# An eight-block performer and mixture-of-experts kernel: the final stage moved beside the last two experts, feature matmuls in 64-row pairs, one one-hot buffer

## The chip, the cores and the metric

The kernel runs on one core of one Trainium2 chip. A core has a matmul engine (TensorE, PE in the tables, with its weight loads as PEld), a vector engine (VectorE, DVE), a scalar engine for activations (ScalarE, ACT), a general engine (GpSimd, POOL) and a queue engine (SyncE, SP). SP, ACT and POOL also issue DMAs. Every engine executes its own queue in order. Matmul results go to PSUM, which has eight banks of 512 float32 columns on 128 partitions; all other tiles lie in SBUF. The metric is the device time of one execution in microseconds (us); the median of several runs is what counts.

## The reference

The input is 4096 tokens of 256 numbers in 8 sequences of 512. Two layers follow, each of the form `x = x + layernorm(f(layernorm(x)))`:

```python
# layer 1: performer attention and an MLP
xp   = einsum('bhnd,md->bhnm', x * norm, proj)      # 16 heads of 16, 64 features
qp   = ratio * (exp(xp - diag - max over m) + eps)          # queries
kp   = ratio * (exp(xp - diag - max over n and m) + eps)    # keys
ctx  = einsum('bhnm,bhnd->bhmd', kp, v)
out  = einsum('bhnm,bhmd->bhnd', qp, ctx) / denom
x    = layer_norm(video + out @ Wo.T + bo, g2, be2)
x    = layer_norm(x + relu(x @ W1.T + b1) @ W2.T + b2, g3, be3)
# layer 2: 8 experts, each takes the 512 tokens that score highest for it
scores = softmax(xf @ gate_w.T)
vals, idx = top_k(scores.T, 512)
y    = layernorm(xf[idx]) * ln_w + ln_b
out  = (gelu(y @ fc1.T + b1s) @ fc2.T + b2s) * vals
xf   = xf.at[idx].add(out)
```

A token may belong to several experts or to none. What leaves the kernel is `x1 + layernorm(xf)` after all experts have added, where `x1` is the result of the first layer.

## The kernel before, in words

The 4096 tokens are worked in NB = 8 blocks of 512; a block has NT = 4 tiles of 128 tokens (t). A scheduler decides the order of the instructions in each engine's queue from the program order and its own estimates; waits are put in wherever a tile, a PSUM bank or a DRAM table is still in use. So the source order and the queue order differ in places.

**Blocks.** Three generators are stepped in turn, so that block b's attention, block b-1's MLP and block b-2's gate are interleaved (L517 to L522). In `attention(b)`, the normalised input is transposed (L159), projected to kT and qT (L231), and the raw features are computed per t: for each half c of the model dimension, one matmul of 128 rows times `pj`, a block-diagonal matrix with 8 copies of proj, into one PSUM bank `px` of 128x512 (L281 for k, L346 for q). DVE reads each bank twice: a maximum (L285, L351) and a subtraction (L286, L353). For k, the maximum over all tokens goes through a POOL reduction (L295) to `nstab`, then ACT takes exponentials (L319), DVE scales them (L323) and PE sums them with v into `pc` (L329). For q, ACT takes exponentials (L357), PE transposes them (`ptq`, L367), ACT copies them out (L372), and PE multiplies with the context (`po`, L382). `mlp(b)` holds the matmuls `ph` (L448) and `pm` (L459); `gate(b)` makes `x1` in SBUF, its layer norm `xf`, which SP stores into the DRAM table `acc` (L478), the gate scores and the rows `yg`, which ACT's queue stores into the DRAM table `xg` (L512).

**PSUM.** Three pools share the eight banks: `ps_mm` (4: matmul results), `ps_tr` (2: transposes), `ps_sm` (2: small results).

**Selection.** A bisection over the scores finds each expert's threshold (L573 to L607); scans give each chosen token a slot. `tokens_of(e)` turns slots into the token list `idx` of an expert: DVE builds a one-hot matrix `hot` of 128x4096 (L662), PE sums it in 32 matmuls into `pi` (L667), DVE makes `idx` from it (L673, L675). `hot` has two buffers.

**Experts.** For expert e, POOL gathers 512 rows from `xg` in four indirect DMAs (L681), PE transposes them, eight matmul pairs `phe` give the hidden layer (L697), ACT applies GELU to each (L702), four groups of 16 PE instructions give `pwe` (L709), DVE adds the bias and multiplies by the kept score (L712, L713), and POOL scatters the four row groups with addition into `acc` (L716). Scatters to one table wait for each other. The weights of expert e+1 are loaded, and its tokens found and gathered, while expert e works.

**Final stage.** After the last scatter, SP loads each of the 8 blocks of `acc` as a tile `z` (L735), the helper `ln_plain` computes its layer norm (DVE statistics L130 and L131, POOL's rs in two instructions L132 and L133, DVE scaling L139), DVE adds `x1` (L739) and ACT's queue stores the block to `out` (L740).

## Time and profile before

| what | value |
|---|---|
| runs | 1170.94, 1167.29, 1170.92, 1169.33 us; median 1170.12 |
| profiled execution | 1166.58 us; span of its work 1164.9 us |
| granted TensorE clock, mean | 0.911 of full |
| blocks, about 30 to 790 us | a block every 94 us or so (transposes from 79.3 to 644.9 us for blocks 1 to 7) |
| selection, about 790 to 860 us | hardly any matmul |
| experts, about 860 to 1106 us | 29.0 us from one expert to the next |
| rest, 1106 to 1165 us | no matmul |

Share of the span by engine: PE 83%, DVE 52%, ACT 24%, POOL 20%. The page of the profile divides the span into 40 slices and gives the busy tenths of each engine:

```profile
PE   2989988998998998899899899882179999999900
DVE  2765467647737737755764773646743110111146
POOL 3010013004103102200300400313042233333222
```

One digit is 29 us. The notch near the 26th digit is the selection; the last two digits are the final stage, in which DVE works and PE doesn't. A mean over the span says little here: each stage has to be read by itself. Matmuls are pipelined, so that a busy PE isn't PE at its peak; where a row gives an engine's idle time, the releaser behind the arrow is the instruction that ended it.

### The profile page before, as it was taken

To read this page: it belongs to the slowest core of one execution; us is meant where nothing else is said; L and a number is where in the kernel's file an instruction comes from. 1 tells how busy PE (TensorE), PEld (TensorE's weight loads), DVE (VectorE), ACT (ScalarE), POOL (GpSimd) and SP (SyncE) were. 2 spreads that over 40 slices of the span, in tenths; PEclk is the share of its full clock that TensorE was granted. 3 is DMA by queue.
4 is the path that set the end of the run, shared out by engine and by line. 5 is a ranking of instruction groups with operands and counts; after the bars stand their busy time and mean duration, and the time that the engine had idled before them with its cause. 6 is when DMAs were issued, how large, how long until landed. Compare 5 with 4: busy or idle time off the path is not lost. (4 is left out here: it accounts for less than half of the span.)

```text
span 1164.9 us, 12047 instructions
## 1 busy us (share of the span) xinstructions
PE 968.2 (83%) x4452; PEld 668.4 (57%) x4452; DVE 602.3 (52%) x1696; ACT 276.0 (24%) x490; POOL 235.2 (20%) x239
## 2 busy tenths in 40 slices
PE   2989988998998998899899899882179999999900
PEld 1575874684585586477458558562047766666600
DVE  2765467647737737755764773646743110111146
ACT  0332332332312323233232241210011121222200
POOL 3010013004103102200300400313042233333222
PEclk9999999998999999999999999895569999999955
DMA  6000001001000100100000010012313434443163
GB/s 223 1 1 1 1 1 49 8 1 36 19 1 0 55 1 1 55 1 1 18 19 1 1 38 1 0 37 84 134 38 91 105 70 108 109 109 73 18 183 115
DMA packets 41177, 52.62 MB, mean 45 GB/s; under 512 B 2720, under 2 KB 37536, under 8 KB 40864
## 3 DMA queue, kind: packets, MB, share of 16 engines
q1 hardware_dynamic: 17248, 24.12, 6.2%
q10 hardware_dynamic: 17728, 19.22, 5.0%
q0 software_dynamic: 6144, 8.52, 4.5%
q8 instruction: 35, 0.57, 0.2%
q14 instruction: 22, 0.18, 0.0%
HBM read 34.95 MB, written 16.91 MB: 45 GB/s over the span
## 5 line engine op out<-in xcount | busy, mean ns | idle before, releaser
L448 PE MATMUL ph<-xaT,w_sb 128*128 128x512 f32 x256 | 131.3, 641 | 20.1 <-DVE kp L286 16.4
L459 PE MATMUL pm<-w_sb,hT 128*128 128x256 f32 x512 | 122.9, 399 | 0.0
L697 PE MATMUL phe<-yT,w1e 128*128 128x512 f32 x256 | 117.8, 620 | 1.6 <-ACT yT L160 1.2
L712 DVE TENSOR_TENSOR o<-pwe,b2s_sb 128x256 f32<-128x256 f32 x32 | 13.6, 425 | 198.8 <-PE pwe L709 198.8
L459 PEld LDWEIGHTS pm<-w_sb,hT 128*128 128x128 f32 x512 | 101.7, 201 | 18.1 <-issue 3.8
L709 PE MATMUL pwe<-w2e,hTe 128*128 128x256 f32 x512 | 111.8, 379 | 0.0
L709 PEld LDWEIGHTS pwe<-w2e,hTe 128*128 128x128 f32 x512 | 97.3, 190 | 16.6 <-issue 3.8
L448 PEld LDWEIGHTS ph<-xaT,w_sb 128*128 128x128 f32 x256 | 51.2, 206 | 83.4 <-issue 71.2
L697 PEld LDWEIGHTS phe<-yT,w1e 128*128 128x128 f32 x256 | 50.2, 199 | 64.1 <-issue 60.5
L716 POOL DMA_INDIRECT acc<-o,idx x32 | 50.4, 1575 | 164.0 <-DVE o L713 75.9
L267 POOL TENSOR_TENSOR xn<-xn,rows_sb 128x1024 f32<-128x1024 f32 x8 | 19.2, 2405 | 303.0 <-PE pt_x L159 303.0
L452 ACT ACTIVATE hT<-ph,cols_sb 128x512 f32<-128x512 f32 x64 | 43.8, 685 | 128.2 <-PE ph L448 121.8
L281 PE MATMUL pxk<-pj,kT 128*128 128x512 f32 x128 | 67.0, 636 | 0.0
L463 DVE TENSOR_TENSOR r<-pm,r 128x256 f32<-128x256 f32 x32 | 13.6, 425 | 101.3 <-PE pm L459 101.3
L329 PEld LDWEIGHTS pc<-v_aug,kp 128*128 128x128 f32 x512 | 61.2, 194 | 6.6 <-issue 3.8
L382 PEld LDWEIGHTS po<-ctxb,qpT 128*128 128x128 f32 x512 | 61.8, 192 | 3.7 <-issue 3.3
L702 ACT ACTIVATE hTe<-phe,cols_sb 128x512 f32<-128x512 f32 x64 | 44.0, 687 | 83.1 <-PE phe L697 83.1
L346 PE MATMUL pxq<-pj,qT 128*128 128x512 f32 x128 | 61.7, 600 | 0.0
L382 PE MATMUL po<-ctxb,qpT 128*128 128x34 f32 x512 | 61.0, 270 | 0.0
L372 ACT ACTIVATE qpT<-ptq 128x512 f32<-128x512 f32 x64 | 34.9, 595 | 108.0 <-PE ptq L367 108.0
L329 PE MATMUL pc<-v_aug,kp 128*128 128x34 f32 x512 | 59.8, 276 | 0.0
L319 ACT ACTIVATE kp<-kp,nstab 128x256 f32<-128x256 f32 x128 | 52.7, 495 | 16.0 <-DVE nstab L297 16.0
(184 smaller groups left out, 1478.9 us busy)
## 6 DMA issues: line engine op xcount, KB each, us to landing
w2e<-in_f ACTq DMA_DIRECT2D x8, 1024.0 KB, 6.0
w1e<-in_f SPq DMA_DIRECT2D x8, 1024.0 KB, 5.2
xg<-yg ACTq DMA_DIRECT2D x8, 528.0 KB, 3.0
x<-in_x_in SPq DMA_DIRECT2D x8, 512.0 KB, 3.9
acc<-xf SPq DMA_DIRECT2D x8, 512.0 KB, 2.8
z<-acc SPq DMA_DIRECT2D x8, 512.0 KB, 6.0
out<-z ACTq DMA_DIRECT2D x8, 512.0 KB, 3.0
w_sb<-in_w SPq DMA_DIRECT2D x2, 1024.0 KB, 12.0
```

What stands on the lines that cost most here:

```text
L281: nc.tensor.matmul(px.rearrange("p h m -> p (h m)"), kT[:, c, ts(t, P)], pj.rearrange("p h m -> p (h m)"), start=True, stop=True,)
L319: nc.scalar.activation(kp[:, :, h, :], kp[:, :, h, :], AF.Exp, bias=nstab[:, h : h + 1])
L329: nc.tensor.matmul(pc[:, hp, :, :].rearrange("p a d -> p (a d)"), kp[:, t, pair, :].rearrange("p h m -> p (h m)"), v_aug[:, t, pair, :].re ...
L346: nc.tensor.matmul(px.rearrange("p h m -> p (h m)"), qT[:, c, ts(t, P)], pj.rearrange("p h m -> p (h m)"), start=True, stop=True,)
L382: nc.tensor.matmul(po[:, 2 * hp : 2 * hp + 2, :].rearrange("p a d -> p (a d)"), qpT[:, hp, :], ctxb[:, hp, :, :].rearrange("p a d -> p (a ...
L448: nc.tensor.matmul(ph, w1_sb[:, c, ts(f, P)], xaT[:, c, :], start=(c == 0), stop=(c == KD - 1),)
L452: nc.scalar.activation(hT[:, f, :], ph, AF.Relu, bias=cols_sb[:, C_B1 + f : C_B1 + f + 1])
L459: nc.tensor.matmul(pw, hT[:, f, ts(t, P)], w2_sb[:, f, :], start=(f == 0), stop=(f == NF - 1),)
L697: nc.tensor.matmul(ph, w1e[:, c, ts(f, P)], yT[:, c, :], start=(c == 0), stop=(c == KD - 1),)
L702: nc.scalar.activation(hT[:, f, :], ph, AF.Gelu_apprx_tanh, bias=cols_sb[:, col : col + 1])
L709: nc.tensor.matmul(pw, hT[:, f, ts(j, P)], w2e[:, f, :], start=(f == 0), stop=(f == NF - 1))
L716: nc.gpsimd.indirect_dma_start(out=acc[:, :], out_offset=bass.IndirectOffsetOnAxis(ap=idx[:, j : j + 1], axis=0), in_=o[:, j, :], in_offse ...
```

## The change

Three parts are changed.

First, the raw features. `pj` holds 8 heads of 16 rows each, so that its rows 0 to 63 are zero in the columns of heads 4 to 7, and rows 64 to 127 in those of heads 0 to 3. The new helper `raw_features` leaves these zero halves out: for each c it issues two matmuls, one from the rows 0 to 63 and one from the rows 64 to 127, each with 256 columns. The two row halves (g) write to two banks of a two-bank tile `pxs`, which comes from a pool of its own, `ps_px`, with two buffers. DVE then reads one bank for each g, as before twice. The views `heads` and `head_cols` put the heads in their old places. To make room in PSUM, `ps_tr` is gone (its tiles come from `ps_mm`), `ps_mm` has 3 banks instead of 4 and `ps_sm` 1 instead of 2.

Second, `hot` has one buffer instead of two.

Third, the final stage. `gate(b)` now also stores `x1` into a DRAM table `x1d` through SP. The experts 6 and 7 (`late`) gather, beside their own rows `y`, the rows of `x1d` and those of `acc` as they stand after all earlier experts (`x1g`, `zg`). After each row group's result `o`, DVE adds it to `zg`, and the layer norm and the addition of `x1g` follow in place; these rows are then scattered to `out` itself, without addition. The blocks are finished as whole blocks from `acc` too: blocks 0 to 3 during expert 6 and blocks 4 to 7 during expert 7, at fixed places in the loops over f and j, with the scaling on ACT instead of DVE (`finish_z`), loads and stores both on SP, and four buffers `z`. The block results are wrong for the rows that experts 6 and 7 still change; the scatters to `out`, which come after the block stores, put the right rows in their place, those of expert 7 after those of expert 6. Expert 7 no longer scatters to `acc`.

```diff
     dram = ctx.enter_context(tc.tile_pool(name="dram", bufs=1, space=DRAM))
-    ps_mm = ctx.enter_context(tc.tile_pool(name="ps_mm", bufs=4, space=PSUM))
-    ps_tr = ctx.enter_context(tc.tile_pool(name="ps_tr", bufs=2, space=PSUM))
-    ps_sm = ctx.enter_context(tc.tile_pool(name="ps_sm", bufs=2, space=PSUM))
+    ps_px = ctx.enter_context(tc.tile_pool(name="ps_px", bufs=2, space=PSUM))
+    ps_mm = ctx.enter_context(tc.tile_pool(name="ps_mm", bufs=3, space=PSUM))
+    ps_sm = ctx.enter_context(tc.tile_pool(name="ps_sm", bufs=1, space=PSUM))
...
     acc = dram.tile([T, D], F32, name="acc")
+    x1d = dram.tile([T, D], F32, name="x1d")
...
         for c in range(KD):
-            pt = ps_tr.tile([P, TB], F32, tag="tr", name=f"pt_{tag}_{c}")
+            pt = ps_mm.tile([P, TB], F32, tag="mm", name=f"pt_{tag}_{c}")
             for t in range(NT):
...
+        HG = HC // 2
+        def heads(t, g):
+            return t.rearrange("p (c g i) m -> p g c i m", c=KD, g=2)[:, g, :, :, :]
+        def head_cols(t, g):
+            return t.rearrange("p (c g i) -> p g c i", c=KD, g=2)[:, g, :, :]
+        def raw_features(qT, t, tag):
+            pxs = ps_px.tile([P, 2, KD, HG, M], F32, tag="px", name=tag)
+            for c in range(KD):
+                for g in range(2):
+                    gs = slice(g * 64, (g + 1) * 64)
+                    nc.tensor.matmul(
+                        pxs[:, g, c, :, :].rearrange("p h m -> p (h m)"),
+                        qT[gs, c, ts(t, P)],
+                        pj[gs, g * HG : (g + 1) * HG, :].rearrange("p h m -> p (h m)"),
+                        start=True, stop=True,
+                    )
+            return pxs
...
             for t in range(NT):
-                for c in range(KD):
-                    hs = slice(c * HC, (c + 1) * HC)
-                    px = ps_mm.tile([P, HC, M], F32, tag="mm", name=f"pxk_{b}_{t}_{c}")
-                    nc.tensor.matmul(
-                        px.rearrange("p h m -> p (h m)"), kT[:, c, ts(t, P)],
-                        pj.rearrange("p h m -> p (h m)"), start=True, stop=True,
-                    )
-                    nc.vector.tensor_reduce(mxk[:, t, hs], px, AX.X, ALU.max)
+                pxs = raw_features(kT, t, f"pxk_{b}_{t}")
+                for g in range(2):
+                    nc.vector.tensor_reduce(
+                        head_cols(mxk[:, t, :], g), pxs[:, g, :, :, :], AX.X, ALU.max
+                    )
                     nc.vector.tensor_tensor(
-                        kp[:, t, hs, :], px,
-                        diagk[:, t, hs].unsqueeze(2).to_broadcast([P, HC, M]),
+                        heads(kp[:, t, :, :], g), pxs[:, g, :, :, :],
+                        head_cols(diagk[:, t, :], g).unsqueeze(3).to_broadcast([P, KD, HG, M]),
                         ALU.subtract,
...
                 qd = a2.tile([P, H, M], F32, tag="qd", name=f"qd_{b}_{t}")
-                for c in range(KD):
-                    hs = slice(c * HC, (c + 1) * HC)
-                    px = ps_mm.tile([P, HC, M], F32, tag="mm", name=f"pxq_{b}_{t}_{c}")
-                    nc.tensor.matmul(
-                        px.rearrange("p h m -> p (h m)"), qT[:, c, ts(t, P)],
-                        pj.rearrange("p h m -> p (h m)"), start=True, stop=True,
-                    )
-                    sh = small.tile([P, HC], F32, tag="sh", name=f"sh_{b}_{t}_{c}")
-                    nc.vector.tensor_reduce(sh, px, AX.X, ALU.max)
-                    nc.vector.tensor_tensor(sh, sh, diagq[:, t, hs], ALU.add)
+                pxs = raw_features(qT, t, f"pxq_{b}_{t}")
+                for g in range(2):
+                    sh = small.tile([P, KD, HG], F32, tag="sh", name=f"sh_{b}_{t}_{g}")
+                    nc.vector.tensor_reduce(sh, pxs[:, g, :, :, :], AX.X, ALU.max)
+                    nc.vector.tensor_tensor(sh, sh, head_cols(diagq[:, t, :], g), ALU.add)
                     nc.vector.tensor_tensor(
-                        qd[:, hs, :], px, sh.unsqueeze(2).to_broadcast([P, HC, M]),
+                        heads(qd, g), pxs[:, g, :, :, :],
+                        sh.unsqueeze(3).to_broadcast([P, KD, HG, M]),
                         ALU.subtract,
...
                 for g in range(2):
-                    pt = ps_tr.tile([P, 4, P], F32, tag="tr", name=f"ptq_{b}_{t}_{g}")
+                    pt = ps_mm.tile([P, 4, P], F32, tag="mm", name=f"ptq_{b}_{t}_{g}")
                     for i in range(4):
...
                 at = ats.pop(t)
-                pt = ps_tr.tile([P, KD, P], F32, tag="tr", name=f"pta_{b}_{t}")
+                pt = ps_mm.tile([P, KD, P], F32, tag="mm", name=f"pta_{b}_{t}")
                 for c in range(KD):
...
             nc.gpsimd.tensor_tensor(x1b, r1, x0, ALU.add)
+            nc.sync.dma_start(
+                x1d[b * TB : (b + 1) * TB, :].rearrange("(t p) d -> p t d", p=P), x1b
+            )
             yield
...
     W = 2 * P
-    pT = ps_tr.tile([P, 2, P], F32, tag="tr", name="pT")
+    pT = ps_mm.tile([P, 2, P], F32, tag="mm", name="pT")
     for k in range(2):
...
-    pv = ps_tr.tile([P, 2, NC // 2, E], F32, tag="tr", name="pslot")
+    pv = ps_mm.tile([P, 2, NC // 2, E], F32, tag="mm", name="pslot")
     for k in range(2):
...
         nc.vector.tensor_scalar(num[:, :, 0, :], num[:, :, 0, :], pcol, None, ALU.mult)
-        hot = ep.tile([P, P, NC], BF, tag="hot", name=f"hot_{e}")
+        hot = ep.tile([P, P, NC], BF, tag="hot", name=f"hot_{e}", bufs=1)
         nc.vector.tensor_tensor(
...
-    def expert(e, idx, y):
+    LATE = 2
+    def rows_of(table, idx, name):
+        g = ep.tile([P, NJ, D], F32, tag=name[:2], name=name)
+        for j in range(NJ):
+            nc.gpsimd.indirect_dma_start(
+                out=g[:, j, :], out_offset=None, in_=table[:, :],
+                in_offset=bass.IndirectOffsetOnAxis(ap=idx[:, j : j + 1], axis=0),
+                bounds_check=T - 1, oob_is_err=True,
+            )
+        return g
+    def scatter(table, idx, j, src, op=None):
+        kw = {} if op is None else {"compute_op": op}
+        nc.gpsimd.indirect_dma_start(
+            out=table[:, :],
+            out_offset=bass.IndirectOffsetOnAxis(ap=idx[:, j : j + 1], axis=0),
+            in_=src, in_offset=None,
+            bounds_check=T - 1, oob_is_err=True, **kw,
+        )
+    def load_z(b):
+        z = ep.tile([P, NT, D], F32, tag="z", name=f"z_{b}", bufs=4)
+        nc.sync.dma_start(
+            z, acc[b * TB : (b + 1) * TB, :].rearrange("(t p) d -> p t d", p=P)
+        )
+        return z
+    def finish_z(b, z):
+        mv, rs = ln_stats(z, NT, f"z{b}")
+        nb = small.tile([P, NT], F32, tag="nb", name=f"nb_{b}")
+        nc.vector.scalar_tensor_tensor(nb, mv[:, :, 0], -1.0, rs, ALU.mult, ALU.mult)
+        for t in range(NT):
+            nc.scalar.activation(
+                z[:, t, :], z[:, t, :], AF.Identity,
+                bias=nb[:, t : t + 1], scale=rs[:, t : t + 1],
+            )
+        nc.vector.tensor_tensor(z, z, x1[:, b * NT : (b + 1) * NT, :], ALU.add)
+        nc.sync.dma_start(
+            out[b * TB : (b + 1) * TB, :].rearrange("(t p) d -> p t d", p=P), z
+        )
+    idxs = {0: tokens_of(0)}
+    ys = {0: gather(0, idxs[0])}
+    zs = {}
+    for e in range(E):
+        if e + 1 < E:
+            ws[e + 1] = load_expert(e + 1)
+            idxs[e + 1] = tokens_of(e + 1)
+            ys[e + 1] = gather(e + 1, idxs[e + 1])
+        idx, y = idxs[e], ys.pop(e)
         w1e, w2e = ws.pop(e)
+        late = e >= E - LATE
+        if late:
+            x1g = rows_of(x1d, idx, f"x1g_{e}")
+            zg = rows_of(acc, idx, f"zg_{e}")
+        if e == E - LATE:
+            for b in range(NB // 2):
+                zs[b] = load_z(b)
         yT = ep.tile([P, KD, CAP], F32, tag="yT", name=f"yT_{e}")
...
+            if late and f in (4, 7):
+                b = (NB // 2 if e == E - 1 else 0) + f // 7
+                finish_z(b, zs.pop(b))
+                if e == E - LATE:
+                    zs[b + 4] = load_z(b + 4)
         o = ep.tile([P, NJ, D], F32, tag="o", name=f"o_{e}")
...
             )
-            nc.gpsimd.indirect_dma_start(
-                out=acc[:, :],
-                out_offset=bass.IndirectOffsetOnAxis(ap=idx[:, j : j + 1], axis=0),
-                in_=o[:, j, :], in_offset=None,
-                bounds_check=T - 1, oob_is_err=True, compute_op=ALU.add,
-            )
-    idxs = {0: tokens_of(0)}
-    ys = {0: gather(0, idxs[0])}
-    for e in range(E):
-        if e + 1 < E:
-            ws[e + 1] = load_expert(e + 1)
-            idxs[e + 1] = tokens_of(e + 1)
-            ys[e + 1] = gather(e + 1, idxs[e + 1])
-        expert(e, idxs[e], ys.pop(e))
-    for b in range(NB):
-        z = ep.tile([P, NT, D], F32, tag="z", name=f"z_{b}", bufs=NB - 2)
-        nc.sync.dma_start(
-            z, acc[b * TB : (b + 1) * TB, :].rearrange("(t p) d -> p t d", p=P)
-        )
-        ln_plain(z, z, NT, f"z{b}")
-        nc.vector.tensor_tensor(z, z, x1[:, b * NT : (b + 1) * NT, :], ALU.add)
-        nc.scalar.dma_start(
-            out[b * TB : (b + 1) * TB, :].rearrange("(t p) d -> p t d", p=P), z
-        )
+            if e < E - 1:
+                scatter(acc, idx, j, o[:, j, :], ALU.add)
+            if late:
+                zj = zg[:, j : j + 1, :]
+                nc.vector.tensor_tensor(zj, zj, o[:, j : j + 1, :], ALU.add)
+                ln_plain(zj, zj, 1, f"l{e}_{j}")
+                nc.vector.tensor_tensor(zj, zj, x1g[:, j : j + 1, :], ALU.add)
+            if e == E - LATE and j in (1, 3):
+                b = 2 + j // 2
+                finish_z(b, zs.pop(b))
+                zs[b + 4] = load_z(b + 4)
+            if e == E - 1:
+                if j in (0, 1):
+                    finish_z(6 + j, zs.pop(6 + j))
+                if j == 1:
+                    for i in range(NJ):
+                        scatter(out, idxs[e - 1], i, zg6[:, i, :])
+                    scatter(out, idx, 0, zg[:, 0, :])
+                if j >= 1:
+                    scatter(out, idx, j, zg[:, j, :])
+        if late:
+            zg6 = zg
...
```

Unchanged lines are left out at "...".

## The prediction

> **What bounds the kernel now.** I read the busy table first, then equal stretches of the span with the busy time of each engine, then the timelines of single engines.
>
> ```profile
> span 1164.9 us, 12047 instructions
> PE 968.2 (83%) x4452; PEld 668.4 (57%) x4452; DVE 602.3 (52%) x1696; ACT 276.0 (24%) x490; POOL 235.2 (20%) x239
> ...
> 330.00:430.00 100.00, 92.31 (x451) 65.55 (x451) 62.11 (x169) 27.70 (x52) 16.30 (x17) 0.96 0.05 17
> 1050.00:1090.00 40.00, 39.71 (x131) 23.99 (x130) 3.46 (x8) 10.70 (x16) 12.01 (x9) 1.00 0.29 55
> 1110.00:1130.00 20.00, 0.00 (x0) 0.00 (x0) 9.80 (x34) 0.00 (x0) 4.11 (x5) 0.50 0.66 201
> 1130.00:1165.00 35.00, 0.00 (x0) 0.00 (x0) 23.29 (x72) 0.00 (x0) 7.60 (x12) 0.50 0.37 129
> ```
>
> The columns after the stretch are PE, weight loads, DVE, ACT and POOL, then the granted clock. Three stages show: the attention and MLP blocks (30 to 790 us), where PE works 92 of 100 us; the experts (860 to 1106), where PE works 39.7 of 40; and a tail without any matmul. PE's last group begins at 1091.81 and takes 13.98, so it ends at 1105.8 and 59.1 us of tail follow. Of these, 8 pass until the last scatter lands, 4 load the first block, and 42.8 (1117.84 to 1160.6) are the eight blocks' statistics, scaling and addition.
>
> ```profile
> 406.82 1.88 PE L346 MATMUL pxq<-pj,qT 128*128 128x512 f32 x4
> 408.54 1.88 PE L448 MATMUL ph<-xaT,w_sb 128*128 128x512 f32 x4
> ...
> 413.74 7.15 PE L459 MATMUL pm<-w_sb,hT 128*128 128x256 f32 x32
> 420.73 1.88 PE L346 MATMUL pxq<-pj,qT 128*128 128x512 f32 x4
> ```
>
> A feature chunk (one t, two matmuls, four PE instructions) holds PE for 408.54 - 406.82 = 1.72 us, 0.43 for 512 columns. A 256-column instruction takes (420.73 - 413.74)/32 = 0.218. Each group is seen 0.16 longer than it holds PE: that is the pipe's emptying, now hidden by the next group.
>
> **The feature matmuls.** There are 8 blocks x 4 t x 2 (k and q) = 64 chunks. Each becomes four matmuls of 64 rows and 256 columns, eight instructions. One after the other they take 8 x 0.218 = 1.75, so nothing is won (+0.03). If the two row halves run at once, neighbours overlap only where the half changes: the order is half 0 twice, half 1 twice, and so on, so eight instructions fill five places, 5 x 0.218 = 1.09, or -0.63. With every pair together it would be 0.87, or -0.85. No matmul of this trace has 64 rows, so this is bounded, not read. Changing between whole and halved arrays may empty the pipe twice, 2 x 0.16 = +0.32. The ends for 64 chunks are thus -0.85 x 64 = -54 and +0.35 x 64 = +22 us. I take five places and one emptying, -0.47 a chunk, since the weight loads (0.19 each, overlapped) leave room for it.
>
> The Trainium skill speaks on both sides in "TensorEngine Tiling (Array Packing)", Key Properties: tiles load and multiply independently, but changing the tiling mode drains the engine. No row here shows either; the first half of the rule would give -54 and the second would add 64 x 0.32 = 20 us to it.
>
> PE time isn't block time. In the k part DVE is the slower one:
>
> ```profile
> 396.24 1.95 PE L448 MATMUL ph<-xaT,w_sb 128*128 128x512 f32 x4 [2.73 <-DVE kp L286]
> ...
> 394.81 0.68 DVE L285 TENSOR_REDUCE mxk<-pxk 128x8 f32<-128x512 f32 x1
> 401.99 0.24 DVE L293 TENSOR_REDUCE mxt<-mxk 128x16 f32<-128x64 f32 x1
> ```
>
> DVE reads the chunks without a gap from 394.81 to 401.99, and only then come the maximum, ACT's exponentials and the matmuls of pc (410.25). Today PE waits 2.73 for a bank in ps_mm; in the changed kernel the features have banks of their own (two chunks), so ph runs on, but chunk 3 must wait until DVE has read chunk 1. In the new DVE order all of yg's statistics stand earlier, which removes most of a 1.25 us wait for rs_g; I let DVE gain about 1.2 there. PE then does chunk 3, pv, ph 6, pxq 0 and ph 7 and reaches pc at about 406.9, 3.3 earlier than now. Behind it the three q chunks lie in dense PE work: 3 x 0.63 = 1.9. Against this, transposes and matmuls now share three banks instead of six and the small results have one instead of two: I charge 0.8 a block, the 0.3 us waits that the pta and pw rows already show, some three more of them. Emptying takes 1.1 (seven chunks at 0.16). That is 3.3 + 1.9 - 0.8 - 1.1 = 3.3 a block, times 7.5 (block 0 starts without MLP work to fill): **-25 us**, with ends -45 and +15, as DVE's chain caps the one and hides some of the other. DVE's two reads (0.69 and 0.68) keep their 512 elements.
>
> **One one-hot buffer.** hot of expert 1 must now wait for pi of expert 0 (846.79 + 2.08 = 848.9), and in the new DVE order idx of expert 0 stands behind it. It was done at 849.44; now 848.9 + 0.2 + 2.28 + 0.15 = 851.5. The gathers, transposes and first expert matmul wait for it: **+2 us**. Later experts compute it a whole expert ahead (29 us), which covers it. Storing x1 (eight DMAs of 512 KB on SP) lies in a queue that waited 439 us for the same x; nothing. x1g's gathers (4 x 1.33) fit POOL's 5.6 idle us before each first scatter.
>
> **The final stage.** The plan moves 47 us of loads and block work beside PE. But the queues run in order, and what stands in front matters:
>
> ```profile
> 1052.73 0.69 ACT L702 ACTIVATE hTe<-phe,cols_sb 128x512 f32<-128x512 f32 x1 [1.03 <-PE phe L697]
> 1054.45 0.69 ACT L702 ACTIVATE hTe<-phe,cols_sb 128x512 f32<-128x512 f32 x1 [1.03 <-PE phe L697]
> ...
> 1054.83 1.56 POOL L716 DMA_INDIRECT acc<-o,idx  x1 [5.51 <-DMA acc<-o,idx]
> 1056.69 1.10 POOL L681 DMA_INDIRECT y<-xg,idx  x1 [0.30 <-issue]
> 1060.76 1.01 POOL L681 DMA_INDIRECT y<-xg,idx  x1 [0.30 <-issue]
> ...
> 1105.59 1.55 POOL L716 DMA_INDIRECT acc<-o,idx  x1 [2.94 <-issue]
> 1110.15 1.55 POOL L716 DMA_INDIRECT acc<-o,idx  x1 [3.00 <-issue]
> ```
>
> In ACT's new queue, block 0's scaling stands between expert 6's second and third GELU. It needs z 0: expert 5's last scatter (1054.83) lands 3.8 later, the load takes 3.9 (1062.5), the statistics 1.8. Its rs then waits on POOL behind four y gathers (to 1061.8) and four zg gathers (1.33 each, to 1067.1), and takes 1.4. So ACT starts at about 1069 what lets the GELU of 1054.45 follow: 15 late. PE fills its three banks to 1057.6 and stands until about 1070; it then meets a slow clock (after the idle time before 861.10 five instructions took 0.85 instead of 0.43, +2.1). Expert 6's second half starts at 1077.5 instead of 1062.83.
>
> Behind it everything hangs on one chain: expert 6's scatters must wait for z 4 and z 5 (whose loads wait for the stores of z 0 and z 1), the third for z 6's load; between them POOL runs seven pairs of rs (1.3 each) that wait for DVE, which waits for PE and ACT. Following the four queues row by row I get expert 6's last scatter at 1112, expert 7's zg at 1120, its PE end at 1126 instead of 1105.8, and then four row groups of some 5.4 each (o 0.42 and 0.35, addition 0.4, statistics 0.5, rs 1.3 with its hand-overs, scaling and addition 0.7, and half a z block of 3 us): last rs at 1141. Only behind it, in POOL's order, stand the eight scatters into out, each waiting for the one before. An adding scatter repeats every 1110.15 - 1105.59 = 4.56; a gather lands in 2.9 (against 3.8), so a plain one costs 3.6 to 4.56: 29 to 36 us. With the 1.3 that today's end has behind its last store, the end is 1171 to 1179 against 1164.9. I take **+10**, ends -20 (no stall in expert 6) and +18.
>
> **Sum:** -25 + 2 + 10 = -13. The profiled execution took 1166.58 (span 1164.9 and 1.7 around it), so 1153.6; the runs' median, 1170.12, is 3.5 above it, so **1157**.
>
> **Rivals.**
> - The halves don't run at once and each change of mode empties the pipe. For it: no row proves overlap. Against: two weight sets in separate rows. Price: 0 to +10 in the blocks, with the tail 1170 + 12 + 5 = 1187; slower as soon as the blocks win less than 12. Chance 0.25.
> - The tail hides as meant: z 0 arrives early enough, PE ends at 1105.8 + 2, then 3.4 for the last rows and eight scatters of 4.1, 33 us: end 1145 by the span, -20; with -25 that is 1125. For it: ACT is busy 10.7 of 40 there. Against: the POOL rows above. 0.12.
> - The blocks are bound by DVE and ACT after all, so the pairs bring only 10, and the tail takes it: 1172. For it: 62 of 100 DVE us, and PE's waits for r and kp (37 us in all). Against: the dense PE rows from 402 to 440. 0.18.
>
> **How the numbers follow.** The forecast has 0.45; its own range is 1142 to 1168. No change means within 0.3% (3.5 us), about what a measurement of this kernel can tell. Faster: 0.43 + 0.12 + 0.03 = 0.58; same: 0.02 + 0.01 + 0.05 = 0.08; slower: 0.24 + 0.10 = 0.34. The range reaches halfway into the fast rival and to the slow one's near side: 1130 to 1184.
>
> **What would show it.** A pxq chunk that holds PE for about 1.1 to 1.25 (1.75 or more: the first rival). ACT idle some 15 us before expert 6's third GELU, released by POOL or DVE, and PE idle after its fifth phe. Eight scatters into out without a gap at the end, 3.6 to 4.6 apart, and PE's end near 1100 in the new span's time. I'm wrong if the blocks' period falls by under 1.5 us or the tail after PE's end is under 35 us.

## The result and the profile after

The changed kernel takes 1173.24 us (median of 51 runs, 1170.44 to 1181.76) against 1169.58 of the kernel before on the same chips (77 runs, 1162.68 to 1176.31). The ratio is 1.0035, 95% interval 1.0025 to 1.0046: slower by 3.7 us or 0.35%, hardly more than the 0.3% that a measurement of this kernel can tell. The forecast was 1157. The profiled execution has a span of 1171.1 us, 6.2 more than before. Executions that took over 1.5% more than the fastest of the same kernel are left out of the times and ratios below.

The first view is again the page's busy table, then stretches of the span (PE, weight loads, DVE, ACT, POOL, granted clock, then the busy share of the DMA engines and GB/s), all of the changed kernel:

```profile
PE 965.3 (82%) x4708; PEld 687.8 (59%) x4708; DVE 608.9 (52%) x1712; ACT 291.4 (25%) x522; POOL 259.4 (22%) x275
...
330.00:430.00 100.00, 93.61 (x490) 68.74 (x489) 64.15 (x173) 27.46 (x51) 15.97 (x17) 0.95 0.07 22
1050.00:1090.00 40.00, 24.59 (x89) 16.68 (x87) 12.05 (x39) 7.71 (x14) 17.35 (x19) 0.83 0.51 142
1110.00:1130.00 20.00, 16.01 (x70) 12.81 (x68) 9.35 (x28) 5.87 (x11) 9.35 (x11) 0.96 0.43 134
1130.00:1165.00 35.00, 0.00 (x0) 0.00 (x0) 8.46 (x25) 2.07 (x4) 10.83 (x14) 0.50 0.17 60
```

In the block stage PE is as full as before but issues 490 matmuls in 100 us where it issued 451, mostly since each feature matmul has become two. In the experts' end (1050 to 1090) PE falls from 39.7 to 24.6 busy us, and matmuls now run until 1126, so that DVE has only 8.5 us of work left in the last stretch instead of 23.3.

The timeline of PE shows that the pairs do what they should; the four lines of two are single moments of the first line, from narrow windows:

```profile
335.07 1.14 PE L268 MATMUL pxq<-pj,qT 64*128 64x256 f32 x8
335.07 0.49 PE L268 MATMUL pxq<-pj,qT 64*128 64x256 f32 x2
335.39 0.38 PE L268 MATMUL pxq<-pj,qT 64*128 64x256 f32 x2
335.60 0.38 PE L268 MATMUL pxq<-pj,qT 64*128 64x256 f32 x2
335.82 0.38 PE L268 MATMUL pxq<-pj,qT 64*128 64x256 f32 x2
336.13 3.72 PE L478 MATMUL pm<-w_sb,hT 128*128 128x256 f32 x16
336.45 0.38 PE L478 MATMUL pm<-w_sb,hT 128*128 128x256 f32 x1
```

A chunk of eight 64-row instructions holds PE for 336.13 - 335.07 = 1.06 us, where four whole ones held it for 1.72. The eight start two by two, within 0.01 us of each other, so they take four places. The middle steps are 0.21 and 0.22, as between two whole matmuls of 256 columns; the first is 0.32, the last 0.31, and the next group's first step, from 336.13 to 336.45, is again 0.32. So each change between 64 and 128 rows loses some 0.1 us on either side of it. The last pm ahead of the chunk starts at 334.76, and from there to 336.45 are 1.69 us; without the two pm (0.22 each) the chunk costs 1.26 instead of 1.72, a gain of 0.46.

So where did the gain go? Marks in PE's timeline divide the two spans (first transposes of block 0 and block 1, the last block's pt_a, the first phe of expert 6, the end):

| piece of the span | before | after | difference |
|---|---|---|---|
| block 0 (first pt_x of block 0 to that of block 1) | 57.3 | 74.8 | +17.5 |
| blocks 1 to 7, up to the last block's pt_a | 665.3 | 642.0 | -23.3 |
| selection and experts 0 to 5 | 304.4 | 305.8 | +1.4 |
| expert 6 to the end | 115.9 | 126.5 | +10.6 |

The sum is +6.2, all that the spans differ by (both start their first transpose at 22.0). The blocks brought nearly what was forecast, the final stage cost nearly what was forecast, and block 0, which the forecast hardly looked at, took three quarters of the gain away. Three stretches of block 0, first of before, then of after:

```profile
36.00:56.00 20.00, 19.68 (x83) 11.95 (x82) 18.01 (x39) 7.35 (x17) 0.40 (x1) 1.00 0.00 1
56.00:68.00 12.00, 12.00 (x91) 10.25 (x89) 6.96 (x19) 4.67 (x8) 0.00 (x0) 1.00 0.00 1
68.00:92.00 24.00, 19.72 (x112) 13.93 (x111) 18.38 (x44) 7.74 (x16) 7.50 (x6) 1.00 0.00 0
```

```profile
36.00:56.00 20.00, 17.57 (x105) 12.36 (x103) 16.78 (x35) 5.94 (x15) 0.39 (x1) 0.91 0.00 1
56.00:68.00 12.00, 12.00 (x50) 9.88 (x50) 3.41 (x10) 4.26 (x7) 0.00 (x0) 0.53 0.00 0
68.00:92.00 24.00, 24.00 (x112) 22.10 (x112) 10.82 (x30) 6.22 (x10) 0.00 (x0) 0.53 0.00 1
```

The third number from the end is the granted clock: 1.00 throughout before, 0.53 from 56 to 92 after (0.50 in each stretch of 4 us from 60 to 88). PE is busy without a gap there, 36 of 36 us, but at half speed; 50 matmuls (of another mixture) pass in 12 us instead of 91. PE's timeline of the changed kernel shows the moment:

```profile
49.89 0.70 PE L268 MATMUL pxq<-pj,qT 64*128 64x256 f32 x4 [1.25 <-DVE kp L309]
52.70 1.08 PE L352 MATMUL pc<-v_aug,kp 128*128 128x34 f32 x8 [0.41 <-DVE kp L346]
54.23 1.97 PE L352 MATMUL pc<-v_aug,kp 128*128 128x34 f32 x16 [0.45 <-DVE kp L346]
56.14 0.75 PE L268 MATMUL pxq<-pj,qT 64*128 64x256 f32 x2
56.82 1.92 PE L352 MATMUL pc<-v_aug,kp 128*128 128x34 f32 x8
59.82 3.63 PE L352 MATMUL pc<-v_aug,kp 128*128 128x34 f32 x16
```

Sixteen matmuls of 34 columns take 1.97 us at 54.23 and 3.63 at 59.82. Neither the busy table nor the waits show this loss: PE is "busy".

### The profile page after: what moved, and what is told of

Its sections match the earlier page's. It is cut to its first block, busy times and chain, and to the rows that moved or that the text cites. A ratio compares the mean times of both kernels' runs of the same rounds, so it can differ in the third digit from the quotient of the medians.

```text
span 1171.1 us, 12633 instructions
## 1 busy us (share of the span) xinstructions
PE 965.3 (82%) x4708; PEld 687.8 (59%) x4708; DVE 608.9 (52%) x1712; ACT 291.4 (25%) x522; POOL 259.4 (22%) x275
## 5 line engine op out<-in xcount | busy, mean ns | idle before, releaser
L467 PE MATMUL ph<-xaT,w_sb 128*128 128x512 f32 x256 | 136.1, 660 | 0.5 <-ACT xaT L161 0.5
L478 PE MATMUL pm<-w_sb,hT 128*128 128x256 f32 x512 | 126.1, 406 | 0.0
L780 PEld LDWEIGHTS phe<-yT,w1e 128*128 128x128 f32 x256 | 50.4, 200 | 81.4 <-issue 57.1
L467 PEld LDWEIGHTS ph<-xaT,w_sb 128*128 128x128 f32 x256 | 48.2, 206 | 50.8 <-issue 44.1
L729 POOL DMA_INDIRECT acc<-o,idx x28 | 45.1, 1610 | 129.6 <-issue 50.1
L401 PEld LDWEIGHTS po<-ctxb,qpT 128*128 128x128 f32 x512 | 65.1, 206 | 8.2 <-ACT qpT L391 4.6
L401 PE MATMUL po<-ctxb,qpT 128*128 128x34 f32 x512 | 67.5, 289 | 1.3
L352 PEld LDWEIGHTS pc<-v_aug,kp 128*128 128x128 f32 x512 | 63.8, 203 | 6.8 <-issue 2.6
L352 PE MATMUL pc<-v_aug,kp 128*128 128x34 f32 x512 | 63.4, 285 | 0.9 <-DVE kp L346 0.9
L376 ACT ACTIVATE qd<-qd 128x1024 f32<-128x1024 f32 x32 | 33.8, 1056 | 113.0 <-DVE qd L371 113.0
L369 DVE TENSOR_REDUCE sh<-pxq 128x8 f32<-128x512 f32 x64 | 43.7, 683 | 15.4 <-PE pxq L268 15.4
```

Of the source, the lines that this page charges most:

```text
L352: nc.tensor.matmul(pc[:, hp, :, :].rearrange("p a d -> p (a d)"), kp[:, t, pair, :].rearrange("p h m -> p (h m)"), v_aug[:, t, pair, :].re ...
L369: nc.vector.tensor_reduce(sh, pxs[:, g, :, :, :], AX.X, ALU.max)
L401: nc.tensor.matmul(po[:, 2 * hp : 2 * hp + 2, :].rearrange("p a d -> p (a d)"), qpT[:, hp, :], ctxb[:, hp, :, :].rearrange("p a d -> p (a ...
L467: nc.tensor.matmul(ph, w1_sb[:, c, ts(f, P)], xaT[:, c, :], start=(c == 0), stop=(c == KD - 1),)
L478: nc.tensor.matmul(pw, hT[:, f, ts(t, P)], w2_sb[:, f, :], start=(f == 0), stop=(f == NF - 1),)
L729: nc.gpsimd.indirect_dma_start(out=table[:, :], out_offset=bass.IndirectOffsetOnAxis(ap=idx[:, j : j + 1], axis=0), in_=src, in_offset=Non ...
```

## The experiments

All ratios are to the kernel before, with runs on the same chip. "Block 0" and "expert 6 to end" are the pieces of the table above, from each run's profiled execution.

| run | median us | ratio, 95% interval | block 0 | blocks 1 to 7 | expert 6 to end |
|---|---|---|---|---|---|
| before | 1169.58 | | 57.3 | 665.3 | 115.9 |
| changed | 1173.24 | 1.0035 (1.0025 to 1.0046) | 74.8 | 642.0 | 126.5 |
| pairs_alone | 1165.68 | 0.9969 (0.9946 to 0.9992) | 80.8 | 643.6 | 115.7 |
| tail_alone | 1178.84 | 1.0072 (1.0045 to 1.0100) | 64.5 | 671.3 | 124.9 |
| whole0 | 1168.40 | 0.9953 (0.9910 to 0.9996) | 73.6 | 642.7 | 124.8 |
| whole_rows | 1193.84 | 1.0179 (1.0099 to 1.0259) | 73.6 | 666.7 | 124.8 |
| filler0 | 1165.91 | 0.9979 (0.9959 to 0.9998) | 67.1 | 645.5 | 125.4 |
| z_on_dve | 1177.23 | 1.0061 (1.0036 to 1.0085) | 78.9 | 643.5 | 127.0 |
| pa_late | 1187.55 | 1.0175 (1.0126 to 1.0223) | 73.4 | 659.5 | 125.5 |
| filler_pa | 1190.98 | 1.0198 (1.0142 to 1.0254) | 68.8 | 663.8 | 126.3 |
| z_later | 1169.61 | 1.0007 (0.9980 to 1.0033) | 74.8 | 642.1 | 123.0 |
| no_e6_out | 1160.50 | 0.9936 (0.9916 to 0.9955) | 73.5 | 642.5 | 113.6 |
| best1 | 1153.78 | 0.9861 (0.9823 to 0.9899) | 68.8 | 643.3 | 108.6 |
| best2 | 1182.88 | 1.0114 (1.0068 to 1.0161) | 72.7 | 664.5 | 109.3 |

The runs of one kernel spread (whole0 from 1156.65 to 1171.09), and one profile is one of them: that of pairs_alone took 1171.7, against its median of 1165.7, and that of tail_alone is the longest of its ten, 1186.9. The pieces of the span show where the time of that execution went; what other executions did there they don't show.

### The parts by themselves: pairs_alone and tail_alone

pairs_alone keeps the old final stage and two one-hot buffers:

```diff
-        hot = ep.tile([P, P, NC], BF, tag="hot", name=f"hot_{e}", bufs=1)
+        hot = ep.tile([P, P, NC], BF, tag="hot", name=f"hot_{e}")
...
-    LATE = 2
...
+    def expert(e, idx, y):
```

> Old final stage and two one-hot buffers, with the changed features and the changed division of PSUM. In the two traces block 0 (first to second block's pt_x) grew from 57.3 to 74.8 us, blocks 1 to 7 shrank by 23.3 in all, expert 6 to the end grew by 10.6. Theory A (block 0 loses its 17.5 us to a granted clock of 0.50 from 56 to 91 us; the final stage costs 10.6 by itself): 1169.6 - 5.8 = 1164, block 0 again near 74.8 with the clock at 0.50 there. Rival B (the slow stretch was an accident of one execution): block 0 near 57, 1147. Rival C (the final stage is free and the loss lies in the blocks): 1173.

Measured 1165.7: the changed features alone make the kernel 0.3% faster, as theory A said, and block 0 is slow here too. B falls; so does C, since expert 6 to end is back at 115.7.

tail_alone is the kernel before with the new final stage, the table x1d and one one-hot buffer:

```diff
-        hot = ep.tile([P, P, NC], BF, tag="hot", name=f"hot_{e}")
+        hot = ep.tile([P, P, NC], BF, tag="hot", name=f"hot_{e}", bufs=1)
...
+    LATE = 2
```

> The features and PSUM of before with the new final stage and one one-hot buffer. Theory A: blocks as before, expert 0 some 2 later, expert 6 stalls about 14 us behind the scaling of block 0 on ACT, and the end comes 10.6 + 2 later: 1182. Rival C (the final stage is free, or gains where the banks are as before: four matmul banks instead of three let PE run one group further): 1165 to 1172.

Measured 1178.8, 0.72% slower, nearer to theory A's 1182 than to C. Expert 6 to end takes 9.0 more than before, and from the last block's last transposes (pt_f) to the first expert's phe it is 64.7 us instead of 62.0 (64.5 in the changed kernel, 62.0 in pairs_alone): the single one-hot buffer costs 2.5 (the stores of x1d come and go with it in these runs; PE's row of pi has a new wait of 2.5 for idx). Unasked, this run shows something else. PE's queue in block 0 is in the order of before, and yet block 0 took 64.5:

```profile
56.00:68.00 12.00, 12.00 (x93) 10.46 (x91) 6.96 (x20) 4.64 (x7) 0.00 (x0) 1.00 0.01 1
68.00:84.00 16.00, 15.48 (x67) 13.56 (x67) 6.46 (x23) 4.43 (x8) 0.00 (x0) 0.52 0.00 0
```

So the slow stretch exists in the old order too, in some executions, and there it follows 12 us in which PE was busy without a gap. In all eight profiles with the new order and no extra work (after, pairs_alone, whole0, whole_rows, z_on_dve, pa_late, z_later, no_e6_out) block 0 takes 73.4 to 80.8. These are eight executions, one of each kernel.

### Rows against order: whole0 and whole_rows

In whole_rows every feature matmul takes all 128 rows again; the banks and the order of all queues remain those of the changed kernel. whole0 does it in block 0 alone (the same line, where b is 0).

```diff
-                    gs = slice(g * 64, (g + 1) * 64)
+                    gs = slice(0, P)
```

> The changed kernel with all 128 rows in all feature matmuls of all blocks: the same instructions, banks and order, but no two halves at once; a chunk holds PE for 1.75 instead of 1.06. Theory A (pairs give PE time in blocks 1 to 7): periods of blocks 1 to 7 grow by 8 x 0.69 less what the waits take up, 3 to 5.5 us each, block 0 as in the run with block 0 whole: 1157 to 1161 plus 21 to 38 = 1180 to 1197. Rival E (the new order and banks gave the 23 us in blocks 1 to 7, DVE sets the period): periods stay near 91: 1157 to 1163.

Measured 1193.8. Blocks 1 to 7 go from 642.0 to 666.7, which is what they took before the change. PE's timeline of this run, with the chunk at 1.72 us again (248.86 - 247.14):

```profile
247.14 1.89 PE L268 MATMUL pxq<-pj,qT 128*128 128x256 f32 x8
248.86 0.38 PE L478 MATMUL pm<-w_sb,hT 128*128 128x256 f32 x1
```

So the halves working at once are worth 24.7 us in blocks 1 to 7, and the new banks and the new order are worth 665.3 - 666.7, nothing within the scatter (tail_alone, with the blocks of before, took 671.3). That is 0.44 for each of the 56 chunks, close to the 0.46 read from the steps above. E falls.

> The changed kernel, in which the feature matmuls of block 0 alone take all 128 rows again (256 columns each, the zero half of pj included; the order of every queue is that of the changed kernel). PE gets 16 x 0.3 = 5 us more work in block 0. Theory A (less work between short waits let the clock fall in block 0): the clock stays near 1 from 56 to 91, block 0 takes 57 to 62, and the whole 1157 to 1161. Rival D (the new division of the banks and the new order cost block 0 its 17.5 us, and the clock only follows): block 0 stays at 75 or grows by up to 5: 1173 to 1178.

Measured 1168.4, between the two theories. In the execution that was traced, block 0 took 73.6 with the clock at half speed again, though PE waited less ahead of it:

```profile
36.00:56.00 20.00, 18.97 (x104) 16.31 (x103) 16.81 (x35) 5.91 (x15) 0.39 (x1) 1.00 0.00 1
56.00:68.00 12.00, 12.00 (x58) 11.42 (x57) 3.53 (x10) 4.30 (x8) 0.00 (x0) 0.57 0.00 0
...
49.93 1.10 PE L268 MATMUL pxq<-pj,qT 128*128 128x256 f32 x4 [0.51 <-DVE kp L309]
54.35 1.97 PE L352 MATMUL pc<-v_aug,kp 128*128 128x34 f32 x16 [0.45 <-DVE kp L346]
```

So giving back the time that the pairs save doesn't keep the clock up each time. But three of the ten executions took 1156.65, 1157.35 and 1160.73, in or next to theory A's 1157 to 1161, with a mean granted clock of 0.894 to 0.897 where the other seven have 0.878 to 0.887. No execution of the changed kernel on record is under 1170.44 or has a clock over 0.886. Some 30 us at half clock, as in the traced execution, are worth 0.013 in that mean, so these three probably ran block 0 without most of the slow stretch; none of them was traced. Theory A is neither shown nor refuted. Rival D has its number in block 0 of the trace, but neither its time nor its reason.

### More work in block 0: filler0

```diff
+            def fill(src, tag):
+                pf = ps_mm.tile([P, HC, M], F32, tag="mm", name=f"pf_{b}_{tag}")
+                nc.tensor.matmul(
+                    pf.rearrange("p h m -> p (h m)"), ident,
+                    src.rearrange("p h m -> p (h m)"), start=True, stop=True,
+                )
...
+                    if b == 0 and hp % 2 == 0:
+                        fill(kp[:, hp // 2, 0:HC, :], hp)
...
+                if b == 0:
+                    fill(qd[:, 0:HC, :], f"q{t}")
```

> The changed kernel with eight more matmuls in block 0 alone, whose results nobody reads (128 rows, 512 columns, moving operand kp or qd, spread over the second half of block 0 in PE's order): 8 x 0.86 = 6.9 us more PE work. In the runs so far block 0 took 57.3 us (before), 64.5 (its blocks with the new final stage), 73.6 to 80.8 (the new banks), and each difference is a stretch at clock 0.50 behind the small matmuls of 34 columns. Theory A2 (the stretch comes from too little work in PE there, whatever the rows): with the extra work the clock stays near 1, block 0 takes 58 to 66, and the kernel 1157 to 1167, faster although it does more. Rival D (the waits of the new order make block 0 long and the clock only shows it): block 0 takes 75 to 82 and the kernel 1173 to 1180.

Measured 1165.9: with 6.9 us of useless matmuls added, the kernel is 0.56% faster than the changed one (ratios 0.9979 and 1.0035), and block 0 takes 67.1. The same three stretches, of this run:

```profile
36.00:56.00 20.00, 17.56 (x106) 12.48 (x105) 17.06 (x36) 6.25 (x15) 0.40 (x1) 0.91 0.01 1
56.00:68.00 12.00, 12.00 (x68) 8.44 (x69) 4.25 (x12) 3.96 (x7) 0.00 (x0) 1.00 0.00 1
68.00:88.00 20.00, 17.38 (x123) 14.28 (x121) 12.42 (x38) 6.64 (x12) 0.00 (x0) 1.00 0.00 0
```

Up to 56 us it is the changed kernel (17.56 busy us against 17.57, clock 0.91 in both); then the clock stays at 1.00. The timeline has the extra matmuls between the small ones:

```profile
56.45 1.99 PE L341 MATMUL pf<-kp,ident 128*128 128x512 f32 x4
58.27 0.98 PE L361 MATMUL pc<-v_aug,kp 128*128 128x34 f32 x8
59.08 1.10 PE L341 MATMUL pf<-kp,ident 128*128 128x512 f32 x2
60.02 1.87 PE L361 MATMUL pc<-v_aug,kp 128*128 128x34 f32 x16
```

Theory A2 holds in the clock and the kernel's time (block 0 is 1.1 over its range), and D falls. How the 17.5 us of block 0 divide is bounded by this run: without the extra matmuls and at full clock the block would take between 67.1 - 6.9 = 60.2, if they lengthen it by all that they take, and 67.1, if they only fill waits. So the new order by itself costs 2.9 to 9.8, and the clock 7.7 to 14.6. tail_alone gives an estimate in between: in the order of before, some 21 us at half clock (0.57 on the mean of 68 to 92) made the block 7.2 longer; the changed kernel's 34 us (0.53 from 56 to 92) would by that cost 12.

The same eight matmuls stand in three more of the traced runs, and there the clock did fall, but came back. In best1:

```profile
56.00:60.00 4.00, 4.00 (x9) 1.77 (x8) 2.90 (x8) 2.67 (x5) 0.00 (x0) 0.58 0.00 0
60.00:64.00 4.00, 4.00 (x26) 3.20 (x27) 0.00 (x0) 0.00 (x0) 0.00 (x0) 1.00 0.00 0
```

filler_pa has the same (0.57, then 1.00; block 0 takes 68.8 in both), best2 0.50 and 0.82, and again 0.59 from 88 to 92 (block 0 takes 72.7). So the extra matmuls shorten the slow stretch in four traces of four, but keep it away in one.

### The start of the other blocks: pa_late and filler_pa

PE waits longer for the layer norm r at each block's start than before, 39.8 us in all instead of 20.4 (the row of pt_a among the groups, before, changed kernel, then pa_late; busy us, mean ns, idle before):

```profile
L159 PE MATMUL pt_a<-ident,r 128*128 128x128 f32 x64 | 15.5, 350 | 20.7 <-DVE r L150 20.4
```

```profile
L160 PE MATMUL pt_a<-ident,r 128*128 128x128 f32 x64 | 16.7, 415 | 39.8 <-DVE r L151 39.8
```

```profile
L160 PE MATMUL pt_a<-ident,r 128*128 128x128 f32 x64 | 15.7, 320 | 18.4 <-DVE r L151 13.0 <-ACT xaT L161 4.1 <-DVE kT L236 0.3
```

```diff
             ln_affine(r1, r1, NT, G2, BE2, f"b{b}")
+            yield
```

> The changed kernel with one more yield between the MLP's layer norm and its transposes, so that in PE's order both pk groups stand ahead of pt_a (now one half of one does). Theory F (PE's 5.2 us wait for r at the start of each block is a latency that other PE work can fill, and the clock falls behind it): the wait falls to 1.5 to 2.5 and blocks 1 to 7 take 2.5 to 4.5 us less each: 1173 - 17 to 1173 - 30 = 1143 to 1156. Rival G (DVE's queue sets the block: kT's eviction now stands ahead of r, r comes later by as much): no gain, 1170 to 1178.

The wait fell as hoped, to 13.0, and blocks 1 to 7 took 17.5 us more: 1187.6. F falls, G is nearest. The edit moves the whole MLP by one step. In blocks 1 to 7 PE is idle 11.8 us less than in the changed kernel (36.5 instead of 48.4), but busy 29.3 more (622.9 instead of 593.6) with the same 3114 matmuls, at a mean clock of 0.93 instead of 0.94. So the loss lies in matmuls that the profile shows longer, not in new waits of PE; why they do stays open.

```diff
             transposed(xnT, xn, f"x{b}")
+            if b > 0:
+                pf = ps_mm.tile([P, TB], F32, tag="mm", name=f"pg_{b}")
+                for kc in (0, 1, 0, 1):
+                    nc.tensor.matmul(pf, ident, xnT[:, kc, :], start=True, stop=True)
```

> The run with eight extra matmuls in block 0 (1165.9), and in each of blocks 1 to 7 four more whose results nobody reads (128 rows, 512 columns, moving operand xnT: 3.4 us), which stand in PE's order between pt_x and pt_a, where PE now waits 5.2 us for r. Theory H (the wait lets the clock fall to 0.50 for some 5.6 us behind it, 2.5 to 2.8 us a block): the wait shrinks to about 1.5, the clock stays up, and the kernel takes 1166 - 7 x 2.5 = 1147 to 1152. Rival I (the clock falls in each block for another reason, the small matmuls of pl or pdk): 1164 to 1168. Rival J (the fillers hold one of three banks, pk comes later): 1170 or more.

Rival J's time: 1191.0. The extra matmuls filled the wait (again 13.0 left), yet blocks 1 to 7 took 18.2 more than in filler0: PE was idle 14.7 less there but busy 32.9 more, of which the 28 extra matmuls, at 0.86 each, are 24. Theory H falls, for the mean clock rose only from 0.94 to 0.95. That the banks are the reason isn't shown. Extra work paid in block 0, which lost 7.7 us or more to the clock, and not here.

### The final stage: z_on_dve, z_later, no_e6_out

Expert 6 stands as forecast, in the timelines of PE and ACT of the changed kernel:

```profile
1067.38 6.90 PE L780 MATMUL phe<-yT,w1e 128*128 128x512 f32 x12 [13.95 <-ACT hTe L785]
```

```profile
1066.15 0.60 ACT L748 ACTIVATE z<-z,nb,rs_z 128x256 f32<-128x256 f32 x1 [17.14 <-DVE nb L746]
1066.66 0.67 ACT L785 ACTIVATE hTe<-phe,cols_sb 128x512 f32<-128x512 f32 x1
```

The GELU of 1066.66 stands behind a scaling that waits 17.14 us for block 0's statistics: z 0 reaches DVE only at 1060.65, and POOL begins its rs, behind four y and four zg gathers, at 1064.52. Two runs take the stall away:

```diff
-        for t in range(NT):
-            nc.scalar.activation(
-                z[:, t, :], z[:, t, :], AF.Identity,
-                bias=nb[:, t : t + 1], scale=rs[:, t : t + 1],
-            )
+        ln_plain(z, z, NT, f"z{b}")
```

> The changed kernel, with the scaling of the finished blocks on DVE (as before the change) instead of ACT. Theory T (expert 6 stands 14 us because its third GELU waits in ACT's queue behind block 0's scaling, which waits for POOL): the wait of PE before expert 6's phe falls from 13.95 to about 1, expert 7 is 10 to 14 earlier, the end follows as far as the serial scatters let it: 1160 to 1168. Rival U (POOL's queue and the late table acc set the end: gathers, rs and scatters keep their places): PE's wait is gone but the last scatter lands when it did: 1171 to 1175.

The wait before phe is gone (1.6 us in the whole run), but waits of 3.9, 6.5 and 4.2 us for DVE's o have come at pwe and pt_y, because DVE now stands in its order behind POOL's rs. Expert 6 to end is 127.0 and the time 1177.2, no gain: nearest to rival U, with the stall moved to another queue.

z_later finishes blocks 0 to 3 with expert 6's four output groups instead of between its GELUs:

```diff
-            if late and f in (4, 7):
-                b = (NB // 2 if e == E - 1 else 0) + f // 7
+            if e == E - 1 and f in (4, 7):
+                b = NB // 2 + f // 7
...
-            if e == E - LATE and j in (1, 3):
-                b = 2 + j // 2
+            if e == E - LATE:
+                b = j
```

> The changed kernel, with the finishing of blocks 0 to 3 moved from between expert 6's GELUs to its four output groups. Theory T (the 14 us stand of expert 6 sits in ACT's order and is what the new final stage loses): the wait before phe is gone, expert 7 starts 8 to 14 earlier and the end follows: 1160 to 1166. Rival U2 (the serial chain of POOL, the z loads and the scatters into acc and out carries the end, so that a stall saved early comes back at expert 7): 1170 to 1175.

Between the two: expert 7 starts at 1082.5 instead of 1095.3 and PE ends 9.6 earlier, but the end comes only 3.5 earlier behind expert 6's start (123.0 instead of 126.5), and 1169.6 is no different from before. So only a third of the stage's loss goes with the stall. POOL's last rows in the timeline of the changed kernel (five of eight scatters left out at the dots):

```profile
1142.49 1.12 POOL L729 DMA_INDIRECT out<-zg,idx  x1 [1.80 <-DMA out<-z]
1145.32 0.99 POOL L729 DMA_INDIRECT out<-zg,idx  x1 [1.71 <-DMA out<-zg,idx]
...
1162.42 0.97 POOL L729 DMA_INDIRECT out<-zg,idx  x1 [2.19 <-issue]
```

Eight scatters, the first released by a block's store and the next six by the one before, start from 1142.49 to 1162.42: 2.85 apart. Behind the last one the span goes on to 1171.1, from 1166 on without any DMA or busy engine.

```diff
-                    for i in range(NJ):
-                        scatter(out, idxs[e - 1], i, zg6[:, i, :])
```

> The changed kernel without the four scatters of expert 6's finished rows into out (those rows of the output keep the block results, which lack the additions of expert 6 and 7). In the trace of the changed kernel the eight scatters at the end repeat every 2.7 to 3.2 us, from 1142.5 to 1162.4, and the span ends at 1171.1. Theory S (the serial scatters are the end's last piece): four fewer take 4 x 2.85 = 11.4 off: 1173.2 - 11.4 = 1162, and the loss of the new final stage against the old one (10.6) is about these four. Rival W (the last rows of expert 7 or the block stores land late and hold the end): 1168 to 1173.

Measured 1160.5, and expert 6 to end 113.6, 12.9 less than with all eight; 1.4 of these are a shorter stall of PE in this execution (12.51 instead of 13.95). S holds: the four scatters of expert 6's rows cost about 11.5 at the very end, more than the stage's net loss of 10.6.

### A version faster than both: best1 and best2

best1 has the pairs, the extra matmuls of block 0, two one-hot buffers and the old final stage with the scaling on ACT and the stores issued by SP instead of ACT:

```diff
-        ln_plain(z, z, NT, f"z{b}")
+        mv, rs = ln_stats(z, NT, f"z{b}")
+        nb = small.tile([P, NT], F32, tag="nb", name=f"nb_{b}")
+        nc.vector.scalar_tensor_tensor(nb, mv[:, :, 0], -1.0, rs, ALU.mult, ALU.mult)
+        for t in range(NT):
+            nc.scalar.activation(
+                z[:, t, :], z[:, t, :], AF.Identity,
+                bias=nb[:, t : t + 1], scale=rs[:, t : t + 1],
+            )
```

> Pairs, the eight extra matmuls in block 0, two one-hot buffers, and the old final stage with one edit: the scaling on ACT instead of DVE, stores on SP. Theory A: pairs with the old final stage took 1165.7; the extra matmuls bring 7.3 as they did with the new one: 1158. DVE's 5.35 us for a block in the old final stage fall by the scaling (4 x 0.4) to about 3.7, eight times 1.65 = 13: 1145. Rival V (the chain DVE to POOL to ACT to DVE or the loads and stores set the period of the final stage): 1153 to 1158.

Measured 1153.8, 1.4% faster than before (1.0 to 1.8) and faster than the changed kernel. Two stretches show where, of before (experts 6 and 7, then the rest) and the same two of best1:

```profile
1049.00:1106.00 57.00, 56.50 (x200) 37.24 (x200) 5.97 (x15) 12.50 (x19) 15.85 (x13) 1.00 0.26 46
1106.00:1165.00 59.00, 0.00 (x0) 0.00 (x0) 33.81 (x106) 0.00 (x0) 12.85 (x18) 0.52 0.46 147
```

```profile
1042.00:1099.00 57.00, 56.50 (x200) 37.25 (x200) 5.65 (x14) 12.68 (x20) 15.79 (x13) 1.00 0.25 47
1099.00:1151.00 52.00, 0.00 (x0) 0.00 (x0) 24.49 (x82) 16.60 (x32) 14.07 (x18) 0.52 0.54 167
```

DVE's share of the rest fell by 9.3 us and the stage by 7.3, less than the 13 expected. The time is in rival V's range; but DVE's waits for POOL's rs, some 1.2 us in each of the eight blocks, are those of before (first block of each):

```profile
1121.10 1.38 DVE L139 TENSOR_SCALAR z<-z,mv_z,rs_z 128x256 f32<-128x256 f32 x4 [1.19 <-POOL rs_z L133]
```

```profile
1114.30 0.16 DVE L773 SCALAR_TENSOR_TENSOR nb<-mv_z,rs_z 128x4 f32<-128x4 f32 x1 [1.19 <-POOL rs_z L133]
```

What was mis-sized is the term itself: a block's scaling held DVE for 1.4, not 1.6, and nb takes 0.2 of it back, so eight blocks save about 9.8 instead of 13. At the end the last addition waits 2.19 for ACT's scaling. The changed kernel for comparison needs 81.4 for the experts and 45.1 for the rest: it saved 14 behind PE and paid 24.6 beside it.

> As the run before it, with the four extra matmuls ahead of pt_a in blocks 1 to 7. Theory H: 17 less than that run, 1128. Rival I: the same as that run, 1145. Rival J: slower than that run.

Measured 1182.9: rival J's sign again, and blocks 1 to 7 take 21.2 more than in best1 (18.2 in filler_pa).

## Why the prediction was wrong

The time lies in the range, on the other side of the forecast: -13 was forecast, +3.7 came.

- **Pairs.** The sum was right, -0.47 a chunk against -0.46 measured, but partly by luck: two of its terms were wrong in opposite directions. Five places and one emptying of 0.16 were charged; the steps show four places of 0.215 (a whole matmul of 256 columns in whole_rows: 1.72 / 8) and some 0.4 for the two changes between 128 and 64 rows. Both halves of the rule from the Trainium skill ("TensorEngine Tiling (Array Packing)", Key Properties) agree with this trace: tiles work at once (pairs that start within 0.01 us), and a change of mode drains the engine (0.1 us lost on either side of each change).
- **Gain of the blocks, "3.3 a block, times 7.5".** For blocks 1 to 7 right: 23.3 measured, 3.3 each. The path to it was different. The wait of ph for kp went from 16.4 to nothing, as said, but the wait of pt_a for r grew by 19.4 where "some three more" waits of 0.3 were charged; and the saved feature time, put at 1.9 + 3.3 a block less 1.1 for emptying, is 3.5 by the comparison with whole rows.
- **The step that failed** is the same sentence's bracket, "block 0 starts without MLP work to fill". It took block 0 to be a block with half the gain, at the clock of before. Having no MLP beside its attention, block 0 consists in its second half mostly of matmuls with 34 and 128 columns. The changed kernel ran it at a clock of 0.53, and block 0 lost 17.5 instead of winning 1.7. That is the whole difference: -13 + 19.2 = +6.2, by which the spans differ (the medians by 3.7). By filler0 at least 7.7 of the 17.5 are the clock, and 2.9 to 9.8 the new order itself. I read the clock as a matter of the experts' start, where I charged 2.1 for it, and nowhere else.
- **One one-hot buffer, +2.** Right: 2.5.
- **Final stage, +10.** Right in sum, 10.6. The stall before expert 6's third GELU was 13.95 (forecast 15) with PE idle until 1067. PE ended 81.4 behind expert 6's start (forecast 77). The eight scatters were mis-sized: 2.85 apart instead of 3.6 to 4.56; eight take 22.8 instead of 29 to 36. Two things took this back: the first scatter starts 97.9 behind expert 6's start, where the last rs was forecast at 92, and the span goes on for 8.7 behind the start of the last scatter, where a scatter and 1.3 had been charged. So the 10 is right partly because errors cancel. That z_later takes the whole stall away and gains 3.5 at the end shows that the stall overlaps with what the other queues do meanwhile: the terms don't add.
- **Rivals.** The halves do run at once, and the tail doesn't hide as meant: it saves 14 behind PE and costs 24.6 beside it. The third rival named the right time, 1172, for a wrong reason: the pairs brought 23, not 10. The two conditions named for being wrong (a period that falls by under 1.5, a tail under 35 us) didn't occur: 3.3 and 45.

What stays open is what lets the clock down in block 0, in all traced executions of the new order without extra work and in one of two of the old. The waits for DVE's late kp between 48 and 55 (1.25, 0.41 and 0.45 us in the changed kernel) don't decide it: filler0 has the same three and holds its clock, whole0 has 0.51 and 0.45 and loses it, and tail_alone loses it after 12 us without a gap. What the runs share is that small matmuls follow. Whether the work that the pairs save matters is undecided, by the three short executions of whole0.

## What to carry to other kernels

Compare the granted clock piece by piece, the first round of a loop above all, for a stretch at half clock looks busy and shows no wait. In block 0 here less work took longer, and eight large matmuls among the small ones made the kernel 0.56% faster; only a run with extra work could tell. One trace is one execution: the mean clock of every execution, on record beside its time, shows what whole0's trace alone hides. Work that is moved beside another stage is paid for in the queues it is put into; price the serial chain that remains at the end first, since here four of its scatters alone were worth more than the stage's whole balance.

## What the runs showed of the hardware

- The clock was 0.50 in each stretch of 4 us from 60 to 88 us of the changed kernel, while PE was busy without a gap. The Trainium skill, in "TensorE: Matmul & The Clock Gate", Part 1 (the clock gate), lets the full clock return after one busy window of about 3.4 us; here eight such windows, mostly of matmuls with 34 and 128 columns, didn't bring it back. The measurement decides: time in which the profile shows PE busy isn't enough. With 6.9 us of 512-column matmuls spread over the stretch it stayed at 1.00 in filler0, and in best1 and filler_pa it fell to 0.58 and 0.57 from 56 to 60 and was back at 1.00 from 60 on.
- One queue order gives different clocks from one execution to the next: block 0 in the order of before took 57.3 at 1.00 and 64.5 with 0.52 from 68 to 84.
- Plain scatters to one table start 2.85 us apart, adding ones 4.56.
- Matmuls on the two row halves of the array overlapped: eight instructions of 64 rows and 256 columns in four places of 0.215 us. Each change between 64 and 128 rows cost some 0.2 us, so that the chunk of 1.72 us became 1.26 and not 0.86.
